# A two-layer attention and convolution block on one core: the projection stage split into two passes over an input kept on chip

## The chip, the cores and the metric

The kernel runs on one core of a Trainium2 chip. The metric is the device time of one execution in microseconds (us); lower is better. Every number of a profile comes from one profiled execution, whose own time is given beside its span.

## The reference

The input `x` is float32 of shape (2, 256, 64, 64), that is two images of 4096 tokens with 256 channels. Layer 0 is global attention, and layer 1 is a gate, a window attention and two 7x7 convolutions. Cut to what matters:

```python
# layer 0: 8 heads of 32 channels, 4096 tokens each
m = resize(mask, (B, 1, 64, 64), "bilinear")             # from 32x32
q, k, v = conv1x1(x, Wq, bq) / sqrt(32), conv1x1(x, Wk, bk), conv1x1(x, Wv, bv)
attn = softmax(q @ k.T); fuse = attn @ v
x = conv1x1(concat([x, fuse]), Wf, bf) * m + x * (1 - m)
# layer 1
x = x * sigmoid(relu(x @ ca_w1 + ca_b1) @ ca_w2 + ca_b2)
x = x + out_proj(window_attention_8x8(x @ qkv_w + qkv_b))   # 4 heads of 64
x = channel_shuffle(x, 4)
y = relu(bn1(grouped_conv7x7(x, sa_w1) + sa_b1))            # 64 groups
return x * sigmoid(bn2(grouped_conv7x7(y, sa_w2) + sa_b2))
```

## The kernel before

**First part.** The work is cut into 16 chunks (2 images x 8) of 512 tokens. For every chunk the loop loads `x` (512 KB, three buffers), and TensorE projects it to q and k (L219) and then to v (L244), each into a PSUM tile of two banks. For each half of q and of k, VectorE adds the bias into an SBUF tile (L230), and ScalarE squares the same PSUM half with the same bias (L231). ScalarE copies v out (L258). SyncE stores q, k and v to DRAM tensors `q_s`, `k_s` and `v_s`, 512 KB each. The squares are summed over the 32 channels of a head by a matmul with a 0/1 matrix `headsum` (L254), and VectorE takes the largest sum of the chunk (L265, tile `nm`). The output tiles q, k and v have two buffers each, so the tile of chunk c is written again in chunk c+2, after its store has landed.

After the last chunk the maxima give a bound on the scores (`top`, `toprow`, `flag`, L269 to L278). If the bound is small, the exponentials need no shift. An `If` on the flag chooses between two copies of the second part; the run takes copy "a".

**Preparation.** The bilinear mask (L152 to L178), the folded batch-norm factors and the convolution weights are made in the same stretch of time, from instructions that stand ahead of the chunk loop or behind it in the program. This part is outside any hand-written order: the framework's scheduler decides where each instruction goes on its engine. GpSimd issues the DMAs of this work, among them 16 writes of zeros to the weight tensor `w_s` (L389, 896 KB each, 14.7 MB in all), the two compact weight tensors `r1_s` and `r2_s` (L392, L396), and zero rows of `x_s` (L403). ScalarE takes the square roots of the variances (L307) and issues the loads of the weights of the later stages (L108).

**Second part.** It is written in a manual order. There are 1024 slots (image, chunk, group of 4 heads, block of 128 keys). In each slot TensorE forms the scores of 4 heads (L580, tile `sa`), ScalarE takes the exponentials (L590, tile `ea`, 8 buffers), TensorE multiplies by v (L609, tile `ava`), and VectorE adds `ea` into a running sum (L611, tile `suma`). The stages of layer 1 are interleaved with later slots, and the convolutions follow at the end. During the slots GpSimd writes one diagonal band of convolution weights into `w_s` every sixth slot (L424, L430). SyncE loads pieces of k and v (`load_piece`, L507 and L509), q (`load_q`, L514), and x and the mask (`load_x`, L520 and L523).

Of the kernel before, what the change touches and what calls it, by code (L numbers as in the profile page):

```python
# [25 lines left out]
HG = 4  # L26
# [28 lines left out]
def conv_seq_kernel(ctx: ExitStack, tc: tile.TileContext, a, out):  # L55
# [50 lines left out]
    def load(name, shape, src, eng, pool=const):  # L106
        t = pool.tile(shape, F32, name=name)
        eng.dma_start(t, src)  # L108
        return t

# [29 lines left out]

    h2 = H // 2
    mhs = []
    mk = ctx.enter_context(tc.tile_pool(name="mk", bufs=2))
    for b in range(B):

        m3 = mk.tile([h2, 3, h2 + 2], F32, tag="m3", name=f"m3_{b}")
        for n in range(3):
            lo, hi = max(0, n - 1), min(h2, h2 + n - 1)  # L150
            at0 = lo - n + 1
            nc.gpsimd.dma_start(  # L152
                m3[at0 : at0 + hi - lo, n, 1 : h2 + 1], a["mask"][b][lo:hi, :]
            )
        nc.gpsimd.dma_start(m3[0:1, 0, 1 : h2 + 1], a["mask"][b][0:1, :])
        nc.gpsimd.dma_start(m3[h2 - 1 : h2, 2, 1 : h2 + 1], a["mask"][b][h2 - 1 : h2, :])
        nc.vector.tensor_copy(m3[:, :, 0:1], m3[:, :, 1:2])
        nc.vector.tensor_copy(m3[:, :, h2 + 1 : h2 + 2], m3[:, :, h2 : h2 + 1])
        mid = mk.tile([h2, h2 + 2], F32, tag="mid", name=f"mid_{b}")
        nc.vector.tensor_scalar_mul(mid, m3[:, 1], 0.75)  # L160
        mv = mk.tile([h2, 2, h2 + 2], F32, tag="mv", name=f"mv_{b}")
        mh = mk.tile([h2, 2, h2, 2], F32, tag="mh", name=f"mh_{b}")
        for o in range(2):
            nc.vector.scalar_tensor_tensor(
                mv[:, o], m3[:, 2 * o], 0.25, mid, ALU.mult, ALU.add
            )
        m75 = mk.tile([h2, 2, h2], F32, tag="m75", name=f"m75_{b}")
        nc.vector.tensor_scalar_mul(m75, mv[:, :, 1 : h2 + 1], 0.75)
        for o in range(2):
            nc.vector.scalar_tensor_tensor(  # L170
                mh[:, :, :, o], mv[:, :, 2 * o : 2 * o + h2], 0.25, m75, ALU.mult, ALU.add
            )
        mhs.append(mh)
    for b, mh in enumerate(mhs):
        for c in range(NCHUNK):
            dst = mask_s[b, c].rearrange("(w r o x) -> o r w x", w=NW, r=4, o=2)
            for o in range(2):
                nc.gpsimd.dma_start(  # L178
                    dst[o],
                    mh[4 * c : 4 * c + 4, o].rearrange("p (w x) t -> p w (x t)", w=NW),  # L180
                )


    nm = const.tile([P, B * NCHUNK], F32, name="nm")
    flag = const.tile([1, 1], I32, name="flag")
    with (
        tc.tile_pool(name="w0", bufs=1) as w0,
        tc.tile_pool(name="x0", bufs=3) as x0,
        tc.tile_pool(name="st0", bufs=2) as st0,
    ):  # L190
        def weight(n):
            return load(n, [P, KC, C], a[n].rearrange("(k p) o -> p k o", p=P), nc.scalar, w0)

        wq, wk, wv = weight("WqT"), weight("WkT"), weight("WvT")
        bias = {}
        for n in ("bq", "bk"):
            t = w0.tile([P, KC], F32, name=n)
            for g in range(KC):
                for j in range(HG):
                    h = HG * g + j  # L200
                    nc.scalar.dma_start(
                        t[32 * j : 32 * j + 32, g : g + 1], a[n][h % 2, :, h // 2 : h // 2 + 1]
                    )
            bias[n] = t

        for b in range(B):
            src = a["x"][b].rearrange("(k p) h w -> p k (h w)", p=P)
            for c in range(NCHUNK):
                x = x0.tile([P, KC, CH], F32, tag="x", name=f"x0_{b}_{c}")
                nc.sync.dma_start(x, src[:, :, c * CH : (c + 1) * CH])  # L210
                sqs = []
                for n, w in (("q", wq), ("k", wk)):
                    s = psum2(f"{n}0_{b}_{c}")
                    for g in range(KC):
                        for kc in range(KC):
                            rhs = x[:, kc, :]
                            if n == "q":
                                rhs = rhs.rearrange("p (r w c) -> p w r c", r=WS, w=NW)
                            nc.tensor.matmul(  # L219
                                s[:, g, :],  # L220
                                w[:, kc, g * P : (g + 1) * P],
                                rhs,
                                start=(kc == 0),
                                stop=(kc == KC - 1),
                            )
                    t = st0.tile([P, KC, CH], F32, tag=n, name=f"{n}st_{b}_{c}")
                    sq = st0.tile([P, KC, CH], F32, tag="sq", name=f"{n}sq_{b}_{c}", bufs=4)
                    bt = bias["b" + n]
                    for g in range(KC):
                        nc.vector.tensor_scalar_add(t[:, g, :], s[:, g, :], bt[:, g : g + 1])  # L230
                        nc.scalar.activation(  # L231
                            sq[:, g, :], s[:, g, :], AF.Square, bias=bt[:, g : g + 1]
                        )
                    sqs += [sq[:, g, :] for g in range(KC)]
                    if n == "q":
                        nc.sync.dma_start(q_s[b, c], t.rearrange("p g n -> p (g n)"))
                    else:
                        for g in range(KC):
                            nc.sync.dma_start(k_s[b, g, c], t[:, g, :])
                s = psum2(f"v0_{b}_{c}")  # L240
                sv = s.rearrange("p a (t o) -> p (a t) o", t=2)
                for m in range(4):
                    for kc in range(KC):
                        nc.tensor.matmul(  # L244
                            sv[:, m, :],
                            x[:, kc, m * P : (m + 1) * P],
                            wv[:, kc, :],
                            start=(kc == 0),
                            stop=(kc == KC - 1),
                        )  # L250

                norms = psum1(f"nrm_{b}_{c}")
                for i, sq in enumerate(sqs):
                    nc.tensor.matmul(  # L254
                        norms[32 * i : 32 * i + 32, :], headsum, sq, start=True, stop=True
                    )
                v = st0.tile([P, KC, 4, P], F32, tag="v", name=f"vst_{b}_{c}")
                nc.scalar.copy(  # L258
                    v.rearrange("p g m d -> p m g d"),
                    sv.rearrange("p m (g d) -> p m g d", g=KC),  # L260
                )
                for g in range(KC):
                    nc.sync.dma_start(v_s[b, g, c], v[:, g].rearrange("p m d -> p (m d)"))
                i = b * NCHUNK + c
                nc.vector.tensor_reduce(nm[:, i : i + 1], norms, AX.X, ALU.max)  # L265


        top = w0.tile([P, 1], F32, name="top")
        nc.vector.tensor_reduce(top, nm, AX.X, ALU.max)  # L269
        row = psum2("toprow")  # L270
        nc.tensor.matmul(row[0:1, 0, 0:P], top, ident, start=True, stop=True)
        qk2 = w0.tile([1, 2], F32, name="qk2")
        nc.vector.tensor_reduce(
            qk2, row[0:1, 0, 0:P].rearrange("p (i r) -> p i r", i=2), AX.X, ALU.max
        )
        prod = w0.tile([1, 1], F32, name="prod")
        nc.vector.tensor_mul(prod, qk2[:, 0:1], qk2[:, 1:2])
        nc.vector.tensor_scalar(flag, prod, (SAFE / SCALE0) ** 2, None, ALU.is_le)  # L278

    wf = load("WfT", [P, 2 * KC, C], a["WfT"].rearrange("(k p) o -> p k o", p=P), nc.scalar)  # L280
    bv = load("bv", [P, KC], a["bv"], nc.scalar)
    bf = load("bf", [P, KC], a["bf"], nc.scalar)
    wqkv = load("qkv_w", [P, KC, 3 * C], a["qkv_w"].rearrange("(k p) o -> p k o", p=P), nc.scalar)
    bqkv = load("qkv_b", [P, 3 * KC], a["qkv_b"], nc.scalar)
    wo = load("out_w", [P, KC, C], a["out_w"].rearrange("(k p) o -> p k o", p=P), nc.scalar)
    bo = load("out_b", [P, KC], a["out_b"], nc.scalar)

    for t in (bqkv[:, 2 * KC : 3 * KC], bo):
        nc.vector.tensor_scalar_mul(t, t, 2.0)
# [13 lines left out]
    def batch_norm(name, t):  # L303
# [9 lines left out]
        return sc, sh  # L313

    cw = ExitStack()
# [897 lines left out]
```

## Time and profile before

| | us |
|---|---|
| median of 3 runs | 3078.66 (3075.16 to 3081.13) |
| the profiled execution's own time | 3070.01 |
| its span, first to last instruction | 3068.2 |
| first matmul of the first part | 5.29 |
| last `nrm` matmul of the first part begins | 208.05 |
| first score matmul of the second part | 219.07 |
| first exponential of the second part | 222.47 |
| first running sum of the second part | 226.56 |
| mean granted TensorE clock | 0.989 |

The span is the time that the profiled execution's instructions cover. Over the whole span TensorE is busy 97%, VectorE 82%, ScalarE 80% and GpSimd 11% of the time. The first part takes about 7% of the span, so these averages say little of it; it must be read from windows of the first 230 us.

### The profile page before, as it was taken

To read this page: it belongs to the slowest core of one execution; us is meant where nothing else is said; L and a number is where in the kernel's file an instruction comes from. 1 tells how busy PE (TensorE), PEld (TensorE's weight loads), DVE (VectorE), ACT (ScalarE), POOL (GpSimd) and SP (SyncE) were. 2 spreads that over 40 slices of the span, in tenths; PEclk is the share of its full clock that TensorE was granted. 3 is DMA by queue.
4 is the path that set the end of the run, shared out by engine and by line. 5 is a ranking of instruction groups with operands and counts; after the bars stand their busy time and mean duration, and the time that the engine had idled before them with its cause. 6 is when DMAs were issued, how large, how long until landed. Compare 5 with 4: busy or idle time off the path is not lost.

```text
span 3068.2 us, 61291 instructions
## 1 busy us (share of the span) xinstructions
PE 2988.2 (97%) x25338; PEld 1015.0 (33%) x25338; DVE 2516.5 (82%) x1398; ACT 2450.6 (80%) x4122; POOL 344.7 (11%) x591
## 2 busy tenths in 40 slices
PE   8989989999999999999999999999999999999897
PEld 4442222232222222222232222323232223224675
DVE  3229989999999999998999999999999998988211
ACT  2239879898989898998989898989898988987423
POOL 7110000001010101010101001010101010000346
PEclk9989999999999999999999999999999999999998
DMA  6953112314141413242322214132413242314264
GB/s 197 356 162 76 59 50 64 67 63 72 59 81 60 75 64 69 66 75 68 66 66 61 66 59 73 59 74 61 78 60 68 70 71 66 109 57 134 61 203 97
DMA packets 160352, 264.20 MB, mean 86 GB/s; under 512 B 43944, under 2 KB 62620, under 8 KB 160064
## 3 DMA queue, kind: packets, MB, share of 16 engines
q1 hardware_dynamic: 133664, 221.72, 24.4%
q0 software_dynamic: 22432, 35.91, 8.4%
q8 instruction: 201, 3.29, 0.4%
q10 hardware_dynamic: 3968, 2.57, 0.3%
q14 instruction: 87, 0.71, 0.1%
HBM read 197.89 MB, written 65.21 MB: 86 GB/s over the span
## 4 chain that ended last, share of the span: by engine, by line
PE 70%; DVE 16%; issue 2%; DMA 2%; ACT 2%; POOL 1%; SPq 0%; DVEq 0%; ACTq 0%; POOLq 0%
PE sa L580 28%; PE ava L609 26%; DVE suma L611 15%; PE qka L748 4%; PE hya L677 4%; PE vwa L834 2%; PE c2a L1011 1%; POOL out_dram L1039 1%; PE c1a L987 1%; ACT ea L590 1%; PE opa L898 1%; DMA out_dram<-za 1%; PE sca L782 1%; PE rda L647 1%; PE pta L857 1%
## 5 line engine op out<-in xcount | busy, mean ns | idle before, releaser
L611 DVE TENSOR_TENSOR suma<-suma,ea 128x2048 f32<-128x2048 f32 x960 | 2198.7, 2290 | 86.0 <-ACT ea L590 1.8
L590 ACT ACTIVATE ea<-sa 128x512 f32<-128x512 f32 (+1 forms) x3072 | 2044.2, 745 | 85.0 <-PE sa L580 36.9
L580 PE MATMUL sa<-qa,ka 32*128 32x512 f32 x8192 | 1189.9, 641 | 8.2 <-DMA ka<-ks 8.0
L609 PE MATMUL ava<-ea,va 128*32 128x512 f32 x8192 | 1092.3, 605 | 0.3 <-ACT fa L619 0.3
L580 PEld LDWEIGHTS sa<-qa,ka 32*128 32x128 f32 x8192 | 333.1, 183 | 762.8 <-ACT ea L590 688.6
L609 PEld LDWEIGHTS ava<-ea,va 128*32 128x32 f32 x8192 | 161.6, 108 | 780.6 <-issue 754.3
L924 POOL DMA_DIRECT2D xs<-xo x94 | 65.9, 708 | 2353.5 <-DVE xo L909 2353.4
L1039 POOL DMA_DIRECT2D out_dram<-za x192 | 108.0, 571 | 128.1 <-DVE za L1033 92.4
L748 PE MATMUL qka<-ua,qkv_w 128*128 128x512 f32 x256 | 118.4, 605 | 0.7 <-DVE ua L738 0.7
L1033 DVE TENSOR_TENSOR za<-za,xla 128x768 f32<-128x768 f32 (+1 forms) x16 | 20.9, 1309 | 101.4 <-ACT za L1027 65.0
L1011 PE MATMUL c2a<-yca,wa 32*128 32x192 f32 (+1 forms) x1400 | 100.0, 427 | 0.3 <-ACT za L1021 0.3
L685 ACT ACTIVATE ta<-hya,bf 128x512 f32<-128x512 f32 x32 | 20.2, 684 | 96.9 <-PE hya L677 96.9
L1011 PEld LDWEIGHTS c2a<-yca,wa 32*128 32x128 f32 x1400 | 91.8, 316 | 10.9 <-issue 9.7
L689 DVE TENSOR_TENSOR ta<-ta,mca 128x512 f32<-128x512 f32 x32 | 22.0, 689 | 88.0 <-ACT ta L685 88.0
L1021 ACT ACTIVATE za<-c2a 128x384 f32<-128x384 f32 (+1 forms) x50 | 26.3, 578 | 79.7 <-DMA out_dram<-za 47.9
L803 ACT ACTIVATE ewa<-ewa,mxwa 128x64 f32<-128x64 f32 x256 | 85.5, 362 | 0.0
L611 DVE TENSOR_TENSOR suma<-ea,ea 128x2048 f32<-128x2048 f32 x32 | 73.1, 2286 | 15.0 <-DMA va<-vs 15.0
L231 ACT ACTIVATE qsq<-q,bq 128x512 f32<-128x512 f32 x32 | 22.0, 687 | 74.1 <-DVE qst L230 72.6
L430 POOL DMA_DIRECT2D ws<-r2s x112 | 69.5, 623 | 68.5 <-DMA xs<-xo 33.2
L761 ACT ACTIVATE qka<-qka,qkv_b 128x512 f32<-128x512 f32 x64 | 40.7, 694 | 44.2 <-PE qka L748 44.2
L987 PE MATMUL c1a<-xla,wa 128*32 128x192 f32 (+1 forms) x896 | 58.7, 413 | 14.2 <-DMA xla<-xs 14.2
L230 DVE TENSOR_SCALAR qst<-q,bq 128x512 f32<-128x512 f32 x32 | 24.0, 751 | 59.1 <-PE q L219 41.2
(139 smaller groups left out, 1674.7 us busy)
## 6 DMA issues: line engine op xcount, KB each, us to landing
ka<-ks SPq DMA_DIRECT2D x256, 256.0 KB
va<-vs SPq DMA_DIRECT2D x256, 256.0 KB
ws<-zero POOLq DMA_DIRECT2D x16, 896.0 KB, 17.1
wa<-ws SPq DMA_DIRECT2D x16, 896.0 KB
xs<-xo POOLq DMA_DIRECT2D x78, 140.0 KB, 7.2
xla<-xs SPq DMA_DIRECT2D x23, 420.0 KB
x<-in_x_dram SPq DMA_DIRECT2D x16, 512.0 KB
ks<-kst SPq DMA_DIRECT2D x32, 256.0 KB
```

The costliest lines, as they stand in the source:

```text
L430: nc.gpsimd.dma_start(band2[:, at0 : at0 + step * (n - 1) + 1 : step, :], spread(r2_s[k : k + 1, :, i], n),)
L580: nc.tensor.matmul(heads[j], k[r, cols], q[r, g, :], start=True, stop=not shifted)
L590: nc.scalar.activation(e[:, h, :], tile, AF.Exp, scale=SCALE0)
L609: nc.tensor.matmul(av[r, :], v[:, m % PB, r], e[:, j, :], start=start, stop=stop)
L611: nc.vector.tensor_add(total, first[0] if m == 1 else total, e)
L677: nc.tensor.matmul(s[:, oc, :], wf[:, kc, oc * P : (oc + 1) * P], xw[kc] if kc < KC else f[:, kc - KC, :], start=(kc == 0), stop=(kc == 2 ...
L748: nc.tensor.matmul(s[:, j, :], wqkv[:, kc, o : o + P], u[:, kc, :], start=(kc == 0), stop=(kc == KC - 1),)
L803: nc.scalar.activation(e[:, n, :], e[:, n, :], AF.Exp, bias=mx[:, n : n + 1], accum_out=rs[:, n : n + 1],)
L924: eng.dma_start(x_s[b, n, p + r0 : p + r1].rearrange("r g w -> g r w"), xo[64 * h : 64 * h + 64, oc, r0 - WS * c : r1 - WS * c, :],)
L987: nc.tensor.matmul(s[32 * j : 32 * j + 32, 0 : n * W], w[:, j, d, :], xs[k][:, 0:n, j, d : d + W], start=(d == 0), stop=(d == KS - 1),)
L1011: nc.tensor.matmul(tiles[j // 2][:, j % 2, 0 : n * W], w[r, d], y[r, 0:n, d : d + W], start=(d == 0), stop=(d == KS - 1),)
L1039: eng.dma_start(dst[b, i, r0:r1, UG * u : UG * u + UG, :], z[p + r0 : p + r1, :, nb * m + n, :],)
```

## The change

All of it is in the first part; the only new line in the second is one ScalarE instruction.

- The loop over chunks is split. Pass 1 makes q and k of all 16 chunks. Pass 2 makes v of all 16. Each chunk of `x` has an SBUF tile of its own (`x0_b_c`, 64 KB of a partition in all), is loaded once, and stays until pass 2. Loads run three chunks ahead.
- The part is inside `tc.manual_schedule()`: every engine executes in the order of the program.
- The squares go to one tile `sq` of 2048 columns. VectorE reduces it by groups of four neighbouring tokens (`tops`, 512 columns). The `headsum` matmuls of chunk i-1 then run on 128 columns instead of 512, behind the projections of chunk i, and the maximum of a chunk is taken over 128 columns.
- Mask, batch norm and weights become a generator `prepare` with some 14 steps. Its first step runs ahead of the loop, and one step follows each chunk. The three square roots are taken together. The zero rows of `x_s` come in step 3; `r2_s` and the 16 zero writes to `w_s` come in the steps behind chunks 10 to 13, in GpSimd's queue behind the last VectorE work on `m2`, which is in the step behind chunk 9.
- The weights of later stages are loaded by ScalarE, four DMAs behind each of the first chunks.
- In pass 2, GpSimd and not SyncE stores v. The last chunk's norms, `flag` and the product `bvf` are made behind v of chunks 0, 1 and 2, not behind the last chunk.
- One exponential of a single element (`warm`) stands at the head of the second part.

The core of the diff (the removed loop is the one described above; the removed preparation has the same operations as the new steps):

```diff
+    pending = []
+    def weight(name, shape, src):
+        t = const.tile(shape, F32, name=name)
+        pending.append((t, src))
+        return t
...
+    def prepare(mk, cwp):
...
+        for b in range(B):
+            for n, r in ((0, 0), (len(BLOCKS) - 1, 31)):
+                for q in range(4):
+                    nc.gpsimd.dma_start(
+                        x_s[b, n, 32 * q + r].rearrange("(p g) w -> p (g w)", g=2),
+                        zero[0 : NG // 2, 0 : 2 * WP],
+                    )
+        yield
...
+        for n in norms:
+            nc.scalar.activation(n[4], n[4], AF.Sqrt)
+        yield
...
+        for i in range(4):
...
+            if i % 2:
+                yield
+        nc.gpsimd.dma_start(
+            r2_s.rearrange("p u i f -> p (u i f)"), m2.rearrange("p u i q x -> p (u i q x)")
+        )
+        for u in range(NU):
+            nc.gpsimd.dma_start(w_s[u], zero)
+            if u % 4 == 3:
+                yield
...
+        def norms(i, tops):
+            s = psum1(f"nrm_{i}")
+            for n in range(2 * KC):
+                s_ = s[32 * n : 32 * n + 32, 0 : CH // 4]
+                nc.tensor.matmul(s_, headsum, tops[:, n, :], start=True, stop=True)
+            nc.vector.tensor_reduce(nm[:, i : i + 1], s[:, 0 : CH // 4], AX.X, ALU.max)
+
+        prepared = prepare(mk, cwp)
+        next(prepared)
+        for _ in range(3):
+            load_chunk()
+        last = None
+        for i, (b, c) in enumerate(chunks):
+            load_chunk()
+            x = xs0[i]
+            sq = st0.tile([P, 2 * KC, CH], F32, tag="sq", name=f"sq_{b}_{c}")
+            tops = st0.tile([P, 2 * KC, CH // 4], F32, tag="top4", name=f"top4_{b}_{c}")
+            for n, w in (("q", wq), ("k", wk)):
...
+                for g in range(KC):
+                    nc.vector.tensor_scalar_add(t[:, g, :], s[:, g, :], bt[:, g : g + 1])
+                    nc.scalar.activation(
+                        sq[:, g + KC * (n == "k"), :], s[:, g, :], AF.Square, bias=bt[:, g : g + 1]
+                    )
...
+            nc.vector.tensor_reduce(
+                tops, sq.rearrange("p g (n f) -> p g n f", f=4), AX.X, ALU.max
             )
+            if i:
+                norms(i - 1, last)
+            last = tops
+            for t, src in pending[4 * i : 4 * i + 4]:
+                nc.scalar.dma_start(t, src)
+            next(prepared, None)
+
+        row = psum1("toprow")
+        top = w0.tile([P, 1], F32, name="top")
+        for i, (b, c) in enumerate(chunks):
+            s = psum2(f"v0_{b}_{c}")
...
+            nc.scalar.copy(
+                v.rearrange("p g m d -> p m g d"),
+                sv.rearrange("p m (g d) -> p m g d", g=KC),
+            )
+            for g in range(KC):
+                nc.gpsimd.dma_start(v_s[b, g, c], v[:, g].rearrange("p m d -> p (m d)"))
+            if i == 0:
+                norms(len(chunks) - 1, last)
+                nc.vector.tensor_reduce(top, nm, AX.X, ALU.max)
...
         banded = bands()
+
+        nc.scalar.activation(warm, ones[0:1, 0:1], AF.Exp)
         load_q(0, 0)
```

## The prediction

> **What bounds the kernel now.** I read first the chain of waits from the start to 300 us, then the timeline of the first part, the waits there, and the DMA queues in stretches of 10 us. From 5.29 to 208.6 us TensorE is almost never idle, so this part looks matmul-bound; undisturbed, a chunk takes 11.51 us (k at 192.5, 204.0: q 3.5, k 3.4, v 3.55, nrm 1.0). 16 x 11.51 = 184, so 19 of its 203 us are lost: 2 at the start, 4.6 and 3.8 where VectorE does batch-norm work (50 to 74 us), 7.4 at 109 to 127, some in other chunks.
>
> What would bind if TensorE did less per chunk shows in the waits (engine, line, what it waited for; us in total, times, longest):
>
> ```profile
> ACT qsq L231 <- DVE qst L230: 72.6, 30, 5.5
> ACT ksq L231 <- DVE kst L230: 32.6, 28, 4.2
> DVE qst L230 <- ACT qsq L231: 12.0, 15, 0.8
> DVE kst L230 <- ACT ksq L231: 10.6, 13, 0.8
> ```
>
> VectorE and ScalarE read the same PSUM tile, and they take turns. One chunk was held up until q and k were both ready; there the turns run at their own pace (start, duration):
>
> ```profile
> 52.97 0.74 DVE L230 TENSOR_SCALAR qst<-q,bq 128x512 f32<-128x512 f32 x1
> 53.81 0.69 ACT L231 ACTIVATE qsq<-q,bq 128x512 f32<-128x512 f32 x1 [1.47 <-DVE bj_sh L312]
> ...
> 54.53 0.75 DVE L230 TENSOR_SCALAR qst<-q,bq 128x512 f32<-128x512 f32 x1
> ...
> 55.20 0.74 DVE L230 TENSOR_SCALAR kst<-k,bk 128x512 f32<-128x512 f32 x1
> ...
> 56.03 0.69 ACT L231 ACTIVATE ksq<-k,bk 128x512 f32<-128x512 f32 x1
> ...
> 56.75 0.75 DVE L230 TENSOR_SCALAR kst<-k,bk 128x512 f32<-128x512 f32 x1 [0.81 <-ACT ksq L231]
> ...
> 57.54 0.69 ACT L231 ACTIVATE ksq<-k,bk 128x512 f32<-128x512 f32 x1 [0.82 <-DVE kst L230]
> ```
>
> From 52.97 to 58.23: **5.26 us per chunk**, whatever TensorE does.
>
> While zeros go to `w_s`, the DMA engines are full. The stretch 90 to 100 us (queue: packets, MB, share) and the stall that follows:
>
> ```profile
> q0 software_dynamic: 462, 2.92, 74.7%
> q1 hardware_dynamic: 463, 1.09, 28.2%
> ```
>
> ```profile
> 115.87 0.75 DVE L230 TENSOR_SCALAR qst<-q,bq 128x512 f32<-128x512 f32 x1 [5.88 <-DMA qs<-qst]
> ...
> 122.27 0.75 DVE L230 TENSOR_SCALAR kst<-k,bk 128x512 f32<-128x512 f32 x1 [4.08 <-DMA ks<-kst]
> ```
>
> VectorE waits 10 us for stores of two chunks earlier. Last, the passage to the second part:
>
> ```profile
> 219.07 3.79 PE L580 MATMUL sa<-qa,ka 32*128 32x512 f32 x14 [7.96 <-DMA ka<-ks]
> ...
> 221.18 1.28 ACT L590 ACT_TABLE_LOAD   x1 [12.43 <-PE sa L580]
> 222.47 3.90 ACT L590 ACTIVATE ea<-sa 128x512 f32<-128x512 f32 x6
> ...
> 226.56 2.29 DVE L611 TENSOR_TENSOR suma<-ea,ea 128x2048 f32<-128x2048 f32 x1 [15.03 <-DMA va<-vs]
> ```
>
> The flag is ready at 211.53, then come the branch (first DMA issued at 212.59, so 1.06), the loads of q and k, cold score matmuls, the table load and six exponentials. From 226.56 on VectorE adds every 2.40 us and falls behind TensorE, which runs at 2.07 per slot until the 8 `ea` buffers are full; so **the start of the first sum sets the start of the rest**.
>
> **What the Trainium skill says.** "PSUM — Partial Sum Buffer", "PSUM bank collisions raise a hardware error", has software keep two engines off the same bank and quadrant, reads against reads included; the trace agrees with the turns above. "VectorE: DVE Perf Modes", "The perf-mode tier table", gives `tensor_reduce` only the 1x mode: agrees, the window maximum (L794) takes 682 ns for 512 elements. "DMA: Bandwidth & Descriptors", "Queues, rings and completion order", has each DMA engine go round its queues packet by packet: agrees, 462 packets against 463, so queue q1 with its smaller packets gets a quarter of the bytes. "TensorE: Matmul & The Clock Gate", "HAM oscillation", warns of idle gaps over some 3.4 us: here after 3.2 us of idling at 120.65 the granted clock is 0.91 over 120 to 140, that is 3.6 us at half speed.
>
> **The change part by part.** I write the new first part as a sum on the scale of the profiled span.
>
> *Start.* The loads of weights and biases on ScalarE's queue are the same, so the first Square comes at 15.4 as before. From there the turns of chunk 0 end 4.4 us later, at 19.8 (5.26 less the 0.84 before the first Square).
>
> *The grouped reduction* is new and has no row. It is 2048 float32 from SBUF in one instruction. L794 has 682 ns for 512 and L611 2290 ns for 2048 in the same mode, so I take 2.28. The groups of four are not shown: from below nothing much (no mode is faster), from above 682 x 4 = 2.7. It starts only behind the last Square (its input), and VectorE's next q stands behind it in program order, so all of it is on the path. Top of chunk 0: 22.2.
>
> *Period of pass 1.* 5.26 + 0.05 (semaphore) + 2.28 + 0.21 for the maximum over 128 columns (279 ns by the row L273, less overlap) = **7.8 us**. TensorE needs 3.5 + 3.4 + 0.25 = 7.2, the quarter-size norms included, so it is no longer the bound; what the smaller norms save (0.75 x 16 = 12 us) comes back as VectorE time. Fifteen more chunks: 22.2 + 117 = 139.2.
>
> *Preparation on VectorE* now stands between chunks, in order, with no cover: two masks at 1.35, biases and identity 0.9, variances 0.35, three reciprocal groups 3.4, `m1` and `cbias1` 1.2, `m2` 1.4, and gaps, together 9.8 by the rows of before (before, most hid under TensorE). Its inputs are early: GpSimd's some 105 small DMAs at 0.6 us, with memsets and waits, end near 72 us, and the first to need them late is at 83. The square roots (1.28 table, 0.7) hide under VectorE's next bias add. 149.0.
>
> *Zero writes.* 14.7 MB behind chunk 9, whose VectorE work ends at 22.2 + 9 x 7.8 + 9.8 = 102. At 0.30 MB per us they last until 152. In this time q1 moves about 0.109 MB per us (1.09 MB above; its packets will be a little larger), so a block of 0.52 MB takes 4.8. The queue holds q10, k10, x14, q11, k11, x15, q12, k12, in this order, from 104.6. q12 lands at 104.6 + 7 x 4.8 + 2 = 140; q of chunk 14 wants its buffer at 133.4: +6.8. k12 lands at 145, wanted at 142.5: +2.5. q13 lands at 150, just in time. I take **9.5**, about what before lost in the same way: 158.5. Loading x three chunks ahead spares no bytes here; x14 and x15 stand ahead of stores that are urgent.
>
> *Pass 2.* v of chunk 0 is done in the stall. The norms of chunk 15 wait for its reduction, and v of chunks 1 to 15 stands behind them on TensorE: 0.3 + 15 x 3.55 + 0.4 (`toprow`) + 1.05 (`bvf`) = 55.0: 213.5. After the stall I add 1.7 for one stretch of half clock. v's copy (1.0) and stores fit under 3.55; the zeros have landed by then. 215.2.
>
> *Passage.* The flag is known some 45 us early, and SyncE, with nothing left to do in pass 2, branches and loads q, k, v into space that waits for no engine; its load of x waits for the last v stores, with the third piece of k and v behind it, not needed for eight slots. So the wait for `ka` (7.96) goes. What is late next is ScalarE: last v copy to 216.4, branch 1.06, table load 1.28 and `warm` 0.2 to 219.0, then six exponentials 3.9: **first sum at 223.0**. The table load is not hidden, it follows the copies. The last v stores (issued at 217.5, about 4 us) land at 221.5, just under it.
>
> *Costed at nothing:* weight DMAs on ScalarE (under the reduction, when it has nothing to do), GpSimd's issue of 32 v stores (0.6 against 1.8 us each), `x0` space. The second part keeps its order.
>
> Sum: 223.0 - 226.56 = -3.6, taken as -3.5. The profiled execution (3070.01, span 3068.2) becomes 3066.5; it lay 8.65 below the median, so the median becomes **3075.2**.
>
> **The rivals.**
> *A, no stall and a cheaper pass 1.* If q1 got 0.15 MB per us or the zeros landed elsewhere, the 9.5 and the half clock vanish: -3.5 - 11 = -14.5, 3064. For it: larger packets in q1, and before lost 7.4, not 10, in TensorE time. Against: 9.4 us of backlog by the queue's own count.
> *B, slower: the reduction by groups of four costs per group.* It writes 512 results where L794 writes 8. If it takes longer than 2.28 + 9.7/16 = 2.9 us the change passes the line of slower; at 3.1 it is 16 x 0.82 = 13 more: 3088. For: no row has short groups. Against: L794 (8 groups) is no dearer than L265 (one group, 691).
> *C, it doesn't do what it says:* the early loads wait after all, at the branch or for space, so 8 us of the passage stay: +4.5, 3083. Against: SyncE's queue has no wait there but DMA lanes.
>
> **How the numbers follow.** About 0.2% (6 us) is what a measurement can tell from no change. My forecast with small errors 0.50, A and gains between 0.30, B 0.13, C 0.07. The forecast's own error is about 5 us (a tenth of a us in the period is 1.6; half a block of queue 2.4), so it gives some 0.04 to each side beyond the line, and C about half of its chance. Faster 0.04 + 0.29 (A, less its smallest gains) = 0.33, slower 0.04 + 0.13 + 0.03 = 0.20, same the rest, 0.47. Range: to A below, 3064, and most of B above, 3087.
>
> **What would show it.** Right: turns at 7.8 us per chunk with TensorE idle about 8% of pass 1 and the grouped reduction near 2.28; VectorE waiting on `qs` and `ks` around chunk 14; pass 1 ending near 158, first score matmul near 217, first sum near 223, no wait on `ka`. Wrong: a period near 7.2 (TensorE still binds), a reduction near 3, zero writes that take q1 less than 9 us, or a first sum outside 212 to 232.

## The result, and the profile after

| | before | changed |
|---|---|---|
| median of 12 runs | 3076.39 us | 3076.44 us |
| lowest to highest | 3070.36 to 3081.46 | 3072.75 to 3083.57 |
| profiled execution (span) | 3070.01 (3068.2) | 3076.63 (3074.8) |
| granted clock, mean | 0.989 | 0.989 |

The ratio of the changed kernel to the one before is 1.0004, 95% interval 0.9993 to 1.0015: no difference that can be measured. An edit that rewrites the first 220 us left the median where it was. The two traces show a gain in the first part and two losses behind it.

The groups of the page after (busy us, mean ns | idle before, what ended it), and the landing time of the zero writes:

```profile
L629 PE MATMUL sa<-qa,ka 32*128 32x512 f32 x8192 | 1186.0, 641 | 7.3 <-DMA ka<-ks 5.9
L660 DVE TENSOR_TENSOR suma<-ea,ea 128x2048 f32<-128x2048 f32 x32 | 73.1, 2284 | 51.3 <-DMA ws<-r2s 51.3
ws<-zero POOLq DMA_DIRECT2D x16, 896.0 KB, 21.7
```

The 51.3 is harmless: VectorE has nothing to do in pass 2. (Its releaser is a guess of the view; the first sum waits for exponentials.) The 5.9 on `ka` is new, and it is not the old wait at the passage.

Pass 1 on VectorE's timeline (start, duration, in brackets the idle time before it):

```profile
28.11 2.29 DVE L450 TENSOR_REDUCE top<-sq 128x512 f32<-128x2048 f32 x1 [0.76 <-ACT sq L442]
35.73 2.29 DVE L450 TENSOR_REDUCE top<-sq 128x512 f32<-128x2048 f32 x1 [0.76 <-ACT sq L442]
...
129.09 0.75 DVE L441 TENSOR_SCALAR qst<-q,bq 128x512 f32<-128x512 f32 x1 [3.56 <-DMA qs<-qst]
135.81 0.75 DVE L441 TENSOR_SCALAR kst<-k,bk 128x512 f32<-128x512 f32 x1 [4.40 <-DMA ks<-kst]
...
144.43 0.75 DVE L441 TENSOR_SCALAR qst<-q,bq 128x512 f32<-128x512 f32 x1 [3.13 <-DMA qs<-qst]
150.08 0.75 DVE L441 TENSOR_SCALAR kst<-k,bk 128x512 f32<-128x512 f32 x1 [3.33 <-DMA ks<-kst]
...
160.71 2.29 DVE L450 TENSOR_REDUCE top<-sq 128x512 f32<-128x2048 f32 x1 [0.75 <-ACT sq L442]
```

The first two lines give the period, 7.62 us. The four waits for stores of q and k add up to 14.4 us, and the last reduction starts at 160.71.

The passage, from the timeline of all engines:

```profile
217.05 1.01 ACT L476 COPY vst<-v 128x1024 f32<-128x1024 f32 x1 [2.44 <-PE v L468]
218.08 1.28 ACT L1141 ACT_TABLE_LOAD   x1
...
221.96 0.38 SPq L569 DMA_DIRECT2D xa<-in_x_dram  x1
...
222.98 2.43 SPq L556 DMA_DIRECT2D ka<-ks  x1
...
223.48 2.29 DVE L660 TENSOR_TENSOR suma<-ea,ea 128x2048 f32<-128x2048 f32 x1 [51.32 <-DMA ws<-r2s]
...
240.31 2.09 PE L629 MATMUL sa<-qa,ka 32*128 32x512 f32 x8 [5.89 <-DMA ka<-ks]
```

The first sum comes at 223.48 (before: 226.56), the gain that was forecast. But the third piece of k is issued at 222.98, behind a load of x that waits for the last stores of v, and TensorE waits for it until 240.31. In the kernel before it was issued earlier, behind a load of x that waited for nothing of the kind, and nobody waited for it:

```profile
217.61 0.61 SPq L507 DMA_DIRECT2D ka<-ks  x1
```

The end of the program, before (first line) and changed:

```profile
3051.42 1.76 DVE L1033 TENSOR_TENSOR za<-za,xla 128x1536 f32<-128x1536 f32 x1 [3.48 <-ACT za L1027]
...
3050.11 13.46 POOL L1088 DMA_DIRECT2D out_dram<-za  x24 [2.88 <-DVE za L1082]
...
3053.30 1.76 DVE L1082 TENSOR_TENSOR za<-za,xla 128x1536 f32<-128x1536 f32 x1 [3.48 <-ACT za L1076]
```

VectorE's last product starts at 3053.30 and the span ends at 3074.8, 21.5 us later. Before, 3051.42 and 3068.2: 16.8. What lies there is an instruction named DRAIN, at the line of the `with` block that holds the whole program. GpSimd's, before and then changed (shortest, median and longest in ns, first and last start):

```profile
L1213 POOLq DRAIN  x3: 46/112/5284, 3062.1 to 3068.0; - x3
L1264 POOLq DRAIN  x3: 46/112/9448, 3064.5 to 3074.6; - x3
```

The long one took 5.28 us before and 9.45 us after, and it also started 0.57 us later behind GpSimd's last store. It does not wait for data on the way: between 3064.6 and 3074 the DMA queues of the changed kernel moved two packets of instructions and nothing else. The busy views don't count it; there it is seen only as an end that comes late.

So, changed minus before, between the two profiled executions: first sum -3.1; from the first to the ninth sum +5.3 (24.85 us instead of 19.51); to the last product -0.4; the end +4.7. Together +6.6, the difference of the spans. The medians show 0.05 (interval about -2 to +5 us), so the parts do not add up to what was measured. The profiled execution of before was a quick one, 6.4 below its median; where it was quick is not known. The profiles do not settle it: from the ninth sum to the last product the fourteen of this document took 2803.5 to 2810.4 us, and before's 2805.4. In all eight kernels with several runs (the changed one and seven below) the first sum, the way to the ninth and the end come together to 0.1 to 5.8 us more, against before's profile, than the ratio shows. The parts show what became faster and what slower; to some us, how they make up the median stays open.

### The profile page after: what moved, and what is told of

It is laid out like the page before. It is cut to its first block, busy times and chain, and to the rows that moved or that the text cites. A ratio compares the mean times of both kernels' runs of the same rounds, so it can differ in the third digit from the quotient of the medians.

```text
span 3074.8 us, 61300 instructions
## 1 busy us (share of the span) xinstructions
PE 2975.1 (97%) x25338; PEld 1013.6 (33%) x25338; DVE 2543.3 (83%) x1413; ACT 2450.5 (80%) x4123; POOL 362.3 (12%) x623
## 4 chain that ended last, share of the span: by engine, by line
PE 76%; DVE 10%; DMA 2%; ACT 2%; issue 1%; POOL 1%; SPq 0%; DVEq 0%; ACTq 0%; POOLq 0%
PE sa L629 31%; PE ava L658 29%; DVE suma L660 9%; PE qka L797 4%; PE hya L726 4%; PE vwa L883 2%; DMA out_dram<-za 1%; PE opa L947 1%; POOL out_dram L1088 1%; PE c2a L1060 1%; ACT ea L639 1%; PE c1a L1036 1%; DVE za L1082 1%; PE sca L831 1%; PE rda L696 1%
## 5 line engine op out<-in xcount | busy, mean ns | idle before, releaser
L660 DVE TENSOR_TENSOR suma<-ea,ea 128x2048 f32<-128x2048 f32 x32 | 73.1, 2284 | 51.3 <-DMA ws<-r2s 51.3
L442 ACT ACTIVATE sq<-q,bq 128x512 f32<-128x512 f32 x32 | 22.0, 687 | 76.5 <-DVE qst L441 71.9
L797 PEld LDWEIGHTS qka<-ua,qkv_w 128*128 128x128 f32 x256 | 46.0, 189 | 72.4 <-issue 58.8
## 6 DMA issues: line engine op xcount, KB each, us to landing
ws<-zero POOLq DMA_DIRECT2D x16, 896.0 KB, 21.7
```

Of the source, the lines that this page charges most:

```text
L660: nc.vector.tensor_add(total, first[0] if m == 1 else total, e)
L797: nc.tensor.matmul(s[:, j, :], wqkv[:, kc, o : o + P], u[:, kc, :], start=(kc == 0), stop=(kc == KC - 1),)
```

## The experiments

Theory 1: the order on SyncE makes the third k piece late. Theory 2: the short packets of the band writes do. Theory 3: the burst of zero writes makes the stall of 14.4 us. Theory 4: the turns of VectorE and ScalarE with the reduction set the period. Theory 5, formed after the first four runs: the stores of v on GpSimd lengthen its DRAIN. Places in the profiles, us. Each ratio is to runs of the kernel before taken beside it (medians 3075.0 to 3076.4). Where there is one run, (1), only the places are read: the 12 runs of either kernel above spread over 11 us.

| run | last reduction starts | first sum | ninth sum less first | last product to end | median (runs), ratio to before |
|---|---|---|---|---|---|
| before | (no such pass) | 226.56 | 19.51 | 16.8 | |
| changed | 160.71 | 223.48 | 24.85 | 21.5 | 3076.44 (12), 1.0004 |
| 1 x late | 160.34 | 224.78 | 19.17 | 21.3 | 3073.13 (14), 0.9994 (0.9985 to 1.0004) |
| 2 bands late | 160.99 | 223.76 | 19.17 | 22.2 | 3072.34 (1) |
| 3 zeros spread | 157.85 | 222.20 | 23.87 | 21.0 | 3077.38 (14), 1.0004 (0.9994 to 1.0014) |
| 4 half reduction | 142.50 | 204.19 | 23.14 | 21.3 | 3054.03 (1) |
| 5 v on SyncE | 161.06 | 232.22 | 19.96 | 16.4 | 3075.61 (14), 1.0004 (0.9993 to 1.0015) |
| 6 half of v on SyncE | 160.63 | 229.90 | 20.55 | 18.0 | 3076.21 (1) |
| 7 before, v on GpSimd | (no such pass) | 215.02 | 19.90 | 21.5 | 3068.10 (1) |
| 8 zeros spread by nm | 145.83 | 210.29 | 20.75 | 21.0 | 3060.05 (10), 0.9956 (0.9944 to 0.9968) |
| 9 last stores on ScalarE | 160.50 | 223.27 | 19.17 | 14.2 | 3066.33 (6), 0.9970 (0.9958 to 0.9982) |
| 10 three edits | 146.10 | 211.86 | 19.16 | 14.2 | 3052.98 (4), 0.9927 (0.9912 to 0.9942) |
| 11 one-bank tiles | 133.52 | 196.86 | 19.16 | 14.6 | 3039.14 (5), 0.9895 (0.9875 to 0.9914) |
| 12 zeros on SyncE | 151.78 | 216.22 | 19.16 | 18.0 | 3062.09 (1) |

### 1. The load of x behind the third piece

```
-        load_x(0, 0)
 ...
             if m % PB == 0:
                 load_piece(i // PB + AHEAD)
+            if i == 1:
+                load_x(0, 0)
```

> The changed kernel with one move: the first attention load of x (which waits for the last stores of v) is issued on SyncE in slot 1 of the loop, behind the third piece of k and v, and no longer in front of it. Theory 1 (the order on SyncE made the third k piece late): the piece is issued near 218 us as in the kernel before, TensorE no longer waits 5.9 us for it near 240, the first running sum stays at 223.5, the ninth comes 5 to 6 us earlier than in the changed kernel, and the time falls by about 5.3 us to 3071 (ratio to the kernel before 0.998). Theory 2 (the short packets of the band writes on GpSimd's queue slow that piece, wherever it is issued): the piece is issued early, but still lands late or its transfer takes over 10 us; a wait of 3 us or more remains and the time stays at 3074 to 3077.

SyncE's timeline shows the third k piece with the other early loads:

```profile
173.20 0.42 SPq L556 DMA_DIRECT2D ka<-ks  x1
```

The wait for `ka` is gone, and ninth less first is 19.17 us, as before the change. Theory 1 holds, in its size too (5.7 us less between those sums). I had expected the issue near 218; it came at 173, since nothing holds SyncE after the branch. The median fell by 3.3 us against the changed kernel's, but the two intervals overlap: of this the trace is the proof, not the median. The first sum came 1.3 us later than in the changed kernel, where I had expected it unmoved.

### 2. The bands late

```
-            if i % 6 == 1:
+            if i > 96 and i % 5 == 1:
                 next(banded, None)
```

> The changed kernel, but the band writes on GpSimd start only after slot 96 instead of at slot 1 (one step in five slots instead of one in six). Theory 1 (order on SyncE): the wait for the third k piece near 240 us stays, at 4 to 7 us, though it may shrink by the part that the transfer itself is slowed (issue 223.0, landing about 240). Theory 2 (contention of the bands' packets): the wait falls below 1 us. The running sums behind it then keep the lead of about 3 us over the kernel before.

```profile
223.26 2.43 SPq L556 DMA_DIRECT2D ka<-ks  x1
...
223.76 2.29 DVE L660 TENSOR_TENSOR suma<-ea,ea 128x2048 f32<-128x2048 f32 x1 [51.32 <-DMA ws<-r1s]
226.15 21.46 DVE L660 TENSOR_TENSOR suma<-suma,ea 128x2048 f32<-128x2048 f32 x9
```

The piece is issued as late as in the changed kernel, and yet nine sums run on without a gap. Theory 2 holds as well. The two don't exclude each other, as I had put it: the piece has slack enough for a late issue or for the bands' traffic, and not for both.

### 3. The zeros spread over pass 1, first form

```
+            if i > 1:
+                pace = st0.tile([1, 1], F32, tag="pace", name=f"pace_{i}")
+                nc.gpsimd.tensor_copy(pace, tops[0:1, 0, 0:1])
+                nc.gpsimd.dma_start(w_s[i - 2], zeros[0])
```

The last two follow in pass 2; the loop at the end of the preparation goes.

> The changed kernel, but the 16 writes of zeros (896 KB each) are issued one per chunk from chunk 2 of pass 1 on, each paced by that chunk's grouped reduction, instead of all behind the last step of the preparation. Theory 3 (the burst of zero writes holds back the stores of q and k, and with two staging buffers VectorE's next turn): the four waits of VectorE for stores of q and k (3.6, 4.4, 3.1 and 3.3 us, 14.4 together) go, the last grouped reduction of pass 1 starts near 147 to 149 instead of 160.7, the first running sum comes at 209 instead of 223.5, and the time falls by about 14 us to 3062 (ratio 0.9955). Rival (the stores of q and k fall behind of themselves, their three queues being as full in any order): waits of 5 us or more remain, spread over more chunks, and the time falls by less than 6 us.

The waits for stores of q and k are gone, and the time is the same. In the waits of the first part two rows carry it:

```profile
POOL pace L459 <- DVE top L448: 64.5, 10, 7.9
DVE top L448 <- POOL pace L459: 12.6, 2, 10.4
```

GpSimd was busy with the preparation's transfers when its pacing copy was due, and that copy reads a buffer that VectorE's reduction two chunks later writes. My edit replaced one wait by another of nearly the same size. It decides nothing on theory 3; experiment 8 paces the zeros another way.

### 4. Half of the reduction

```
-                tops, sq.rearrange("p g (n f) -> p g n f", f=4), AX.X, ALU.max
+                tops[:, 0:KC], sq[:, 0:KC].rearrange("p g (n f) -> p g n f", f=4), AX.X, ALU.max
```

The maxima of q are then used for both, so the bound that picks the branch leaves k out.

> The changed kernel with the grouped reduction of pass 1 over q's half alone (1024 elements a partition instead of 2048); it leaves the part of k out of the bound that picks the branch, so it is a measurement of pass 1 and no version of the kernel. Theory 4 (the turns of VectorE and ScalarE over the pairs plus the reduction, in one chain, set the period of 7.62 us; TensorE's 7.2 is beside them): the reduction takes 1.15 us, the period falls to TensorE's 7.2 or a little over, and the 9.8 us of preparation on VectorE is partly hidden. Rival (TensorE with its order q, k, norms is itself the bound): the period stays within 0.1 us of 7.62.

```profile
46.57 1.21 DVE L450 TENSOR_REDUCE top<-sq 128x256 f32<-128x1024 f32 x1
53.99 1.21 DVE L450 TENSOR_REDUCE top<-sq 128x256 f32<-128x1024 f32 x1
61.41 1.21 DVE L450 TENSOR_REDUCE top<-sq 128x256 f32<-128x1024 f32 x1
```

In these chunks the period is 7.42 us, with preparation steps between (others are at 6.66, where VectorE catches up on work that TensorE has ready). The first sum came 19.3 us earlier although the stall for stores grew to 20.2 us (2.0, 5.5, 4.4, 5.1 and 3.2). Theory 4 holds: the reduction was on the path of every chunk. The rival, TensorE as the bound, stands only 0.2 us behind.

### 5. All stores of v on SyncE

Experiment 1, and:

```
-                nc.gpsimd.dma_start(v_s[b, g, c], v[:, g].rearrange("p m d -> p (m d)"))
+                nc.sync.dma_start(v_s[b, g, c], v[:, g].rearrange("p m d -> p (m d)"))
```

> The kernel of the first experiment (x behind the third piece), with the 32 stores of v in pass 2 issued on SyncE as in the kernel before, and no longer on GpSimd. In four profiles of the changed kernel and its variants GpSimd's last wait before the end (a DRAIN behind its last store of the result) takes 9.45 us, in that of the kernel before 5.28; GpSimd issues 591 transfers against 559, and the 32 more are these stores. Theory 5 (the stores of v on GpSimd's queue lengthen that wait): it falls to about 5.3 us, and the time falls by about 4.2 us against the first experiment, to 3069 (ratio to the kernel before 0.998). Rival (the wait's length comes from something else that the change moved, such as the order of the writes of zeros and bands): it stays at 9 to 10 us and the time at 3073.

The DRAIN fell to 4.63 us and the end to 16.4: theory 5 holds for the wait. The time did not fall, a miss. The waits of the first 260 us show two rows of their own:

```profile
ACT vst L476 <- DMA vs<-vst: 17.9, 6, 6.2
...
PE sa L629 <- DMA ka<-ks: 7.1, 1, 7.1
```

ScalarE's copies wait for stores of v, TensorE waits for `ka` at the passage again, and the first sum came at 232.22, 7.4 us later than in experiment 1. Where the stores are issued has a price at both ends.

### 6. Half of them

```
+                eng = nc.sync if g else nc.gpsimd
+                eng.dma_start(v_s[b, g, c], v[:, g].rearrange("p m d -> p (m d)"))
```

> The kernel of the first experiment with 16 of the 32 stores of v on SyncE (g = 1) and 16 left on GpSimd, 575 transfers on GpSimd. If each transfer on GpSimd adds its share to the last wait (4.17 us over 32, 0.13 us each), the wait takes about 7.4 us. If it goes by a step (a part of the queue that is closed or not), it takes 5.3 or 9.5 us. If it doesn't depend on these stores, 9.5.

5.94 us: more than the 4.63 of experiment 5, less than the 7.4 of a proportional share. Neither form that I had named.

### 7. The kernel before with v on GpSimd

The same one-word edit as in experiment 5, the other way round, in the kernel before.

> The kernel before, with nothing changed but the engine that issues its 32 stores of v: GpSimd for SyncE. Theory 5: GpSimd's last wait grows from 5.28 us to about 9.45 us and the time from its last instruction on VectorE to the end of the span by about 4.2 us, with no pass split and no order changed. Rival (the wait comes from the order of the other writes): it stays at 5.3 us.

The DRAIN took 9.69 us, the end 21.5: the engine of these 32 stores alone does it. I had not expected the first sum at 215.02, 11.5 us earlier than before and 8.5 us earlier than in the changed kernel: in these profiles this one word did more for the first part than the whole change. GpSimd's timeline has a cause to suggest:

```profile
77.22 1.60 POOL L389 DMA_DIRECT2D ws<-zero  x3
83.74 1.59 POOL L389 DMA_DIRECT2D ws<-zero  x3
95.35 2.11 POOL L389 DMA_DIRECT2D ws<-zero  x4
106.87 1.59 POOL L389 DMA_DIRECT2D ws<-zero  x3
```

In the kernel before, nine zero writes went out in a row at 72. Here the stores of v stand between them in GpSimd's order and wait for their chunk, so the zeros come three or four to a chunk. That fits theory 3. So would the 8.4 MB of v that SyncE's queue no longer carries; no further run took the two apart.

### 8. The zeros spread, paced by nm

As experiment 3, but the pacing copy stands behind `norms` and reads a column that is never written again:

```
+                nc.gpsimd.tensor_copy(pace, nm[0:1, i - 1 : i])
```

> The changed kernel with the 16 writes of zeros spread over pass 1 again, each now paced by the column of nm of the chunk before (a buffer that is not reused), so that VectorE's grouped reduction no longer waits for GpSimd's pacing copy, which cost 12.6 us in the third experiment. Theory 3: the waits for the stores of q and k (14.4 us) stay away, no other wait takes their place, the last grouped reduction starts near 147 us, the first running sum comes at 208 to 211 us, and the time falls by 12 to 14 us to about 3063 (ratio 0.996). Rival (the zeros, paced through the whole pass, hold back the stores a little in every chunk): waits of 5 us or more in sum, first running sum at 213 or later.

The writes of zeros land in 7.2 us (median of those whose landing the trace shows) instead of 21.7, the queue of the stores moved 8.56 MB from 100 to 152 us (5.31 in the changed kernel), no wait for `qs` or `ks` is left in the first 260 us, and no engine waits for the pacing. VectorE keeps its period to the end of pass 1:

```profile
138.21 2.29 DVE L448 TENSOR_REDUCE top<-sq 128x512 f32<-128x2048 f32 x1 [0.75 <-ACT sq L440]
145.83 2.29 DVE L448 TENSOR_REDUCE top<-sq 128x512 f32<-128x2048 f32 x1 [0.75 <-ACT sq L440]
```

First sum at 210.29, 13.2 us earlier than in the changed kernel; median 3060.05, ratio 0.9956. Theory 3 holds, its rival falls.

### 9. The last item's stores on ScalarE

Experiment 1, and:

```
                             eng = nc.sync if i >= 2 else nc.gpsimd
+                            if i < 2 and k == len(items) - 1:
+                                eng = nc.scalar
```

> The kernel of the first experiment (x behind the third piece) with the 12 stores of the last item's result that GpSimd issues moved to ScalarE's queue, which is idle there. Theory 5 (GpSimd's last wait, 9.45 us since it also stores v, follows its own last transfer and lies on the end of the span): GpSimd ends some 7 us earlier, its wait is covered by the last item's stores, the time from VectorE's last product to the end falls from 21.2 us to 13 to 15 us, and the time falls by 6 to 8 us to 3066 (ratio to the kernel before 0.997). Rival (the wait is for the last stores to land, whoever issues them): it ends as late as before, the time from the last product to the end stays at 19 us or more, the time at 3073.

```profile
3042.77 6.73 POOL L1090 DMA_DIRECT2D out_dram<-za  x12 [2.89 <-DVE za L1082]
3045.96 1.76 DVE L1082 TENSOR_TENSOR za<-za,xla 128x1536 f32<-128x1536 f32 x1 [3.48 <-DMA out_dram<-za]
3047.75 6.74 ACTq L1090 DMA_DIRECT2D out_dram<-za  x12
```

GpSimd's last transfer is now one item earlier, and its DRAIN (8.49 us) runs beside the last stores. From the last product to the end 14.2 us instead of 21.3; ratio 0.9970 against 0.9994 in experiment 1, and the two intervals do not overlap. The rival (a wait for the last stores to land) falls. The DRAIN still ends last, at 3059.3 of 3060.2.

### 10. Three edits together

Experiments 1, 8 and 9 in one kernel.

> Three edits together: x behind the third piece, zeros spread by nm, last item's stores on ScalarE. If their effects add: the eighth-experiment time of 3060 less 1.5 us for what was left of the wait for the third k piece less 6 to 8 us at the end, 3051 to 3053 (ratio 0.992 to 0.993). If the wait for the k piece was an answer to bands and zeros alone, the order of x brings nothing more: 3054.

Median 3052.98: the effects add, as forecast.

### 11. One bank to a tile

Experiment 10, and q and k of pass 1 in tiles of one PSUM bank:

```
-    psum_layout("0", 3, 2)
+    psum_layout("0", 2, 4)
...
-                s = psum2(f"{n}0_{b}_{c}")
+                s = [psum1(f"{n}0_{b}_{c}_{g}") for g in range(KC)]
```

`s[:, g, :]` becomes `s[g]`.

> The kernel of the three edits, with q and k of pass 1 in PSUM tiles of one bank (four of them, and two pairs left for v) instead of tiles of two banks. Theory 4 (VectorE and ScalarE take turns on a tile of two banks although they work on different banks, and these turns with the reduction set the 7.6 us of a chunk): with a tile for each bank VectorE works on one while ScalarE works on the other, TensorE sets the period (6.7 us in the run with half the reduction), the preparation is hidden beside it, the last grouped reduction of pass 1 starts near 122 to 128 us instead of 147, the first running sum comes near 186 to 190, and the time falls by 20 to 24 us to about 3030 (ratio 0.985). Rival (the turns are inherent in reading PSUM from two engines, or the stores of q and k, now faster, run full again): the period stays above 7.4 us or waits for stores of q and k come back, and the gain is under 8 us.

The windows of two undisturbed chunks (us, busy us and count of PE, PEld, DVE, ACT, POOL, clock, DMA share, GB/s):

```profile
118.68:126.10 7.42, 7.42 (x25) 3.12 (x24) 5.30 (x6) 2.66 (x4) 0.70 (x2) 1.00 0.97 389
126.10:133.52 7.42, 7.42 (x28) 3.57 (x27) 5.30 (x7) 2.66 (x4) 0.71 (x2) 1.00 0.69 275
```

and of one in experiment 10:

```profile
107.98:115.60 7.62, 6.74 (x24) 2.77 (x23) 5.30 (x6) 2.72 (x4) 1.24 (x3) 1.00 0.82 297
```

TensorE is busy all of 7.42 us: it is the bound again. The two readers overlap, in the first of these chunks from 121.92 to 122.48:

```profile
121.08 1.40 DVE L439 TENSOR_SCALAR qst<-q,bq 128x512 f32<-128x512 f32 x2
...
121.92 1.29 ACT L440 ACTIVATE sq<-q,bq 128x512 f32<-128x512 f32 x2 [3.27 <-DVE qst L439]
```

More buffering is not the reason: q and k have four single banks here, shared with the norms, where they had three pairs. The last reduction starts 12.6 us earlier than in experiment 10: 15 x 0.2 = 3.0 from the period, and the rest, 9.6, from preparation that is now hidden. The gain, 13.8 us in the median, is short of the 20 to 24 that I expected, since I had read 6.7 as TensorE's period out of chunks where VectorE was catching up. Two signs of the rival came, a period above 7.4 and waits for stores of k (2.3 and 1.7 us), but TensorE did not stop for these, and the gain is above the rival's 8. At 0.9895 (0.9875 to 0.9914) this version is about 1% faster than the kernel before.

### 12. The zeros on SyncE

Experiment 1, and `nc.sync` for `nc.gpsimd` in the loop of zero writes.

> The kernel of the first experiment with the 16 writes of zeros issued on SyncE instead of GpSimd; all 32 stores of v stay on GpSimd, which issues 575 transfers, as many as with half of the stores of v moved. If the number of GpSimd's transfers sets its last wait: about 5.9 us, as there. If the stores of v themselves do: it stays at 9.4 us. In pass 1 the zeros now stand in SyncE's order before the stores of q and k and its loads of x: the stall of 14.4 us stays or grows.

The DRAIN took 5.96 us: as long as with 16 stores of v taken away (experiment 6), though all of these stayed. It goes with the number of GpSimd's transfers in these runs, whichever they are, and not with their bytes (40.1 MB in GpSimd's queue in experiment 6, 29.6 here):

| transfers on GpSimd | DRAIN, us |
|---|---|
| 559 | 5.28 (before), 4.63 (exp. 5) |
| 575 | 5.94 (6), 5.96 (12) |
| 579 | 8.49, 8.47, 8.47 (9, 10, 11) |
| 591 | 9.45 (changed, 1, 3, 4, 8), 9.69 (7), 10.10 (2) |

It is not linear: 2.5 us lie between 575 and 579, where the last transfers differ too. What it works off is open. My other expectation missed: the stall shrank, to 2.4 and 3.4 us:

```profile
135.41 0.75 DVE L441 TENSOR_SCALAR qst<-q,bq 128x512 f32<-128x512 f32 x1 [2.37 <-DMA qs<-qst]
...
146.55 0.75 DVE L441 TENSOR_SCALAR qst<-q,bq 128x512 f32<-128x512 f32 x1 [3.41 <-DMA qs<-qst]
```

On SyncE the zeros also no longer go out in a burst. Its order puts four of them behind the stores of each of four chunks:

```profile
107.38 3.30 SPq L326 DMA_DIRECT2D ws<-zero  x4
...
115.95 5.57 SPq L326 DMA_DIRECT2D ws<-zero  x4
...
126.64 6.31 SPq L326 DMA_DIRECT2D ws<-zero  x4
...
136.96 6.39 SPq L326 DMA_DIRECT2D ws<-zero  x4
```

So this run changed the queue and the pacing together, and does not show which of them made the stall shorter.

## Why the prediction was right or wrong

The forecast was 3075.2 against 3078.66, a gain of 3.5 us, too small to be told from none; measured was no change. The number stood nearer than the reasoning: the first part came out as summed to half a us, partly by errors that cancel, and two losses behind it had been costed at nothing. In the profiles these lose 10.0 us where the first part gains 3.1. That the median did not rise with them is not explained, and so the forecast had luck.

- **Start:** the first Square came at 16.34, not 15.4. ScalarE issues the loads of the biases itself; it was done with them at 15.02 (14.09 before) and then loaded its table. The end of the first reduction: 23.0 against 22.2. "The first Square comes at 15.4 as before" was not so.
- **Grouped reduction:** 2286 ns against 2.28 us. Groups of four cost nothing extra, so rival B fell. This agrees with the one mode that the Trainium skill ("VectorE: DVE Perf Modes", "The perf-mode tier table") gives the operation.
- **Period:** 7.62 against 7.8; the turns were the bound. TensorE needs 7.42 (experiment 11), not 7.2, so it was a close second. On the turns themselves the prediction says that the trace agrees with the skill's page "PSUM — Partial Sum Buffer" ("PSUM bank collisions raise a hardware error"), but that page keeps two engines apart only on the same bank and quadrant. The turns here also kept them apart on the two banks of one tile; with a tile for each bank they overlap (experiment 11). What imposes the turns on a tile of two banks is not shown.
- **Preparation:** 9.8 uncovered us were forecast; the first twelve periods show 102.3 - 12 x 7.62 = 10.9.
- **Zero writes:** the mechanism was right, the size off: 14.4 us for 9.5. The term that was too small is "a block of 0.52 MB takes 4.8". From 100 to 152 us the queue of the stores moved 5.31 MB, 0.102 per us instead of 0.109, so a block took 5.1 or more, and chunks came faster (7.62). The waits began at chunk 13, not 14: its q waited until 129.1 for the store of q11, which the prediction's count has landed at 104.6 + 4 x 4.8 + 2 = 125.8. Chunk 15 did not wait; "q13 lands at 150, just in time" held.
- **Pass 2:** 3.45 us per chunk against 3.55, and no half clock, for which 1.7 us had been added. That came earlier, inside the stall: the granted clock was 0.56 over 140 to 145 us and 0.50 over 155 to 160, and 1.00 again from 165 on. From the end of the last reduction (163.0) to the last copy (218.06) 55.1 us, where the prediction had 57.9.
- **Passage:** the wait for `ka` of 7.96 us went, as said. The branch's 1.06 us did not show on ScalarE: table load at 218.08, right behind the last copy. First sum 223.48 against 223.0: 4.5 late at the end of pass 1, 2.8 and 1.2 early in pass 2 and the passage.
- **Costed at nothing, first:** "its load of x waits for the last v stores, with the third piece of k and v behind it, not needed for eight slots". This step failed. The wait was named, its cover was not priced: the slots in hand from 218 on lasted to 234.4, and a piece issued at 223 needed 17.2 us (the chain) beside the band writes. It cost 5.3 us; without the late issue, or without the band writes, it cost nothing (experiments 1 and 2).
- **Costed at nothing, second:** "GpSimd's issue of 32 v stores". The issue was free; what they did to GpSimd's DRAIN 2800 us later cost 4.2 us, and its later start 0.6.
- **Rivals:** A named the right prize: with the zeros spread (experiment 8), 3060 against its 3064. C fell, SyncE's loads went early (169 us).

## What to carry to other kernels

A moved transfer has three prices: its issue, what stands behind it in its queue, and what it adds at the end of the program. Pace bulk writes that nobody waits for by the work they run beside, with a signal in a buffer that is not reused. Where two engines read one PSUM tile of two banks in turns, try a tile for each bank; here that took 13.8 us off.

## What the runs showed of the hardware that was not expected

- GpSimd's DRAIN at the end took 4.6 to 10.1 us, longer with more transfers of GpSimd in the program (559 to 591), even when 32 of them had been issued 2800 us before. With 12 stores moved to ScalarE's queue, which issued them in 6.74 us like GpSimd (6.73), the end came 7 us earlier.
- The same 14.7 MB of zeros cost pass 1 14.4 us of waits when GpSimd issued them in a burst, 5.8 when SyncE issued them four to a chunk, and none when GpSimd issued one to a chunk.
